# ScalarE's square-root table, the routers' weights on another DMA queue, and products of the identity on TensorE in the first ten microseconds of a transformer block

## The chip, the cores and the metric

The kernel runs on one core of a Trainium2 chip. The metric is the device time of one execution in microseconds. A core has five engines that each work through a queue of instructions in order: TensorE (PE, matmuls and, as PEld, weight loads), VectorE (DVE), ScalarE (ACT), GpSimd (POOL) and SyncE (SP, which here only issues DMAs). ACT and POOL issue DMAs too. In the profile, L110 is line 110 of the kernel.

## What is computed

The reference is one layer in float32 on x of 16 batches, 512 tokens, 256 features. It normalizes each token, and adds to x a linear attention (feature map elu + 1, 16 heads) and a mixture of experts: a shared expert, and 8 routed ones in 2 groups, of which each token takes 2.

```python
xn = _layernorm(x, axis=-1)
x = x + _L0_attn_ref(xn, Wq, bq, Wk, bk, Wv, bv, Wo, bo) \
      + _L0_ffn_ref(xn, w_in, w_out, w1, w2, wg, we, gb, eb)
...
# in _L0_attn_ref
q, k = feature_map(xn @ Wq + bq), feature_map(xn @ Wk + bk)
kv = einsum('bkhd,bkhm->bhdm', k, v)
out = einsum('bqhd,bhdm->bqhm', q, kv) / max(einsum('bqhd,bkhd->bqh', q, k), 1e-6)
...
# in _L0_ffn_ref
g_probs = softmax(flat @ wg.T + gb); e_logits = flat @ we.T + eb
```

`we` (8 columns) and `wg` (2 columns) are the routers' weights.

## The kernel before, in words

A batch of 512 tokens is four tiles of 128 tokens (NT = 4). For every batch the kernel normalizes the tokens (`xn`), brings them into transposed form (`xnT`, the features on the partitions), multiplies by keys and routers in one go (`wkr_sb`: 256 columns of wk, 8 of we, 2 of wg, so 266), then by the queries' weights, and goes on to attention, to the hidden layers of both experts, and to the routing. The main loop (L1034) is staggered: in the turn of batch b the front of batch b + 1 is made (L1038), batch b + 2 is normalized (L1058, `normalize`, statistics at L283), and batch b + 3 is loaded. After all batches, a last stage gathers the tokens of each pair of experts and multiplies them by the second layer (L993).

The change lies in the start:

- L106 `load_x` issues a batch's tokens on SP's queue. L130 loads batch 0 in four pieces, one a tile; L164 loads batch 1 whole, and L1033 batch 2, behind all weights on SP's queue.
- L143 to L145 load we, wg and wk into `wkr_sb`, issued by ACT. L147 takes a square root of a constant, so that the square root's table is loaded early (in the profile a row ACT_TABLE_LOAD of L147).
- L149 loads wq on SP's queue; L151 to L162 load the biases on POOL's; L178 to L193 load the other weights on SP's.
- L300 `first` makes batch 0's and batch 1's start. `measure` (L318) takes mean and variance of a tile on DVE. `scale` takes the root on ACT (L325, `sd`), its inverse and the normalized tile on DVE (L326, L328). `place` (L332) transposes a tile by two products with the identity on PE (L335) and copies it by ACT (L338). `keys` and `queries` are the matmuls through `times` (L342), and `keep` (L355) adds the bias to a result on DVE. L359 to L378 write out their order: tile by tile `measure`, `scale` and the `place` of the tile before, then `keys(0)`, the last tile's `place`, the other keys, the queries, and then the same for batch 1.
- L385 `residual` adds the output bias to the tokens on POOL (L390), and L393 `feature_map` ends in L402.
- The front of batch 1 is `project` (L404): keys at L412, their bias at L416, L417, queries at L423. `summarize` (L684) multiplies the normalized tokens by batch 0's keys (L689); `first_rows` (L636) and `first_hidden` (L655) are the hidden layers of batch 0.

What is passed through `keep_in_program_order` (`pin` in `first`) stays behind what was written before it for its engine. All other instructions are put in order by the compiler's planner, which works with its own estimate of when data come. The semaphores between engines are made by the compiler as well.

Two lines set which instruction of batch 2 stands in DVE's queue early:

```python
with tc.issue_after(last_xn[-1].ins) if last_xn else nullcontext():
    for t in range(g, g + n):
        nc.vector.bn_stats(out=st[:, t, :], in_=xt[:, t, :])
```

So the statistics of batch 2 have to come behind batch 1's last normalized tile, and where behind it is up to the planner.

Of the kernel before, what the change touches and what calls it, by code (L numbers as in the profile page):

```python
# [10 lines left out]
FP = mybir.dt.float32  # L11
# [4 lines left out]
P = 128  # L16
# [5 lines left out]
def block_kernel(  # L22
# [29 lines left out]
    nc = tc.nc  # L52
    B, S, D = x.shape
    G = wg.shape[1]
    E = we.shape[1]
# [5 lines left out]
    NT = S // P  # L61
# [28 lines left out]
    ps_y = ctx.enter_context(tc.tile_pool(name="ps_y", bufs=2, space=bass.MemoryType.PSUM))  # L90
# [12 lines left out]

    hs_all = keep.tile([P, KH, S], FP, name="hs_all")

    def load_x(b, pieces=1):  # L106
        xt = x_all[:, b % 2]
        n = NT // pieces
        for i in range(pieces):
            tc.keep_in_program_order(nc.sync.dma_start(  # L110
                out=xt[:, ts(i, n), :], in_=x[b, ts(i, n * P), :].rearrange("(t p) d -> p t d", p=P)
            ))
        return xt


# [6 lines left out]
    def by_quadrant(a):  # L122
        return a.rearrange("p (q c i) -> p c q i", q=NQ, i=Q)
# [3 lines left out]
    ident = const.tile([P, P], FP)  # L127
    make_identity(nc, ident)

    xs = {0: load_x(0, NT)}  # L130
    KR = D + E + G
    wkr_sb = wp.tile([P, KD, KR], FP)


    w2_sb = wp.tile([P, KH, G * NL * D], FP)
# [3 lines left out]
        first = (LATE + 2 * (i % 2)) * D  # L139
        return w2_sb[:, i // 2, first : first + n * HID]  # L140


    nc.scalar.dma_start(out=wkr_sb[:, :, D : D + E], in_=we.rearrange("(p c) e -> p c e", p=P))  # L143
    nc.scalar.dma_start(out=wkr_sb[:, :, D + E : KR], in_=wg.rearrange("(p c) e -> p c e", p=P))
    nc.scalar.dma_start(out=wkr_sb[:, :, 0:D], in_=wk.rearrange("(p c) f -> p c f", p=P))  # L145
    root = const.tile([P, 1], FP)
    tc.keep_in_program_order(nc.scalar.activation(root, eps_sb, AF.Sqrt))  # L147
# [9 lines left out]
    for q in range(NQ):  # L157
        nc.gpsimd.dma_start(
            out=bv_sb[ts(q, Q)], in_=bv[ts(q, KD * Q)].rearrange("(c i) -> i c", i=Q)
# [3 lines left out]
    if B > 1:  # L163
        xs[1] = load_x(1)  # L164
# [17 lines left out]
    for k in range(KD):  # L182
        for c in range(KD):
            nc.sync.dma_start(
                out=wv_sb[:, k, ts(c, P)].rearrange("p (q i) -> p q i", i=Q), in_=by_quadrant(wv[ts(k, P), :])[:, c]
            )
    wo_sb = wp.tile([P, KD, D], FP)
    for q in range(NQ):
        nc.sync.dma_start(
            out=wo_sb[ts(q, Q)], in_=wo[ts(q, KD * Q), :].rearrange("(c i) d -> i c d", i=Q)  # L190
# [4 lines left out]
    def load_expert(i):  # L195
# [13 lines left out]
        out=headmask, in_=ones, pattern=[[-DH, P // DH], [0, DH]],  # L209
# [3 lines left out]
        out=headmask, in_=headmask, pattern=[[DH, P // DH], [0, DH]],  # L213
# [5 lines left out]
        out=before, in_=ones, pattern=[[1, P]],  # L219
# [80 lines left out]
    def first():  # L300

        pin = tc.keep_in_program_order
        stats = []
        for b in range(2):
            stats.append([
                small.tile([P, NT, n], FP, tag=tag, name=f"{tag}_{b}")  # L310
                for tag, n in (("st", 6), ("mv", 2), ("sd", 1), ("rs", 1))
            ])
        kk, qq = kk_all[:, 0], qq_all[:, 0]
        lg = small.tile([P, NT, E + G], FP, tag="lg", name="lg_0")
        xnT = [work.tile([P, KD, S], FP, tag="xnT", name=f"xnT_{b}") for b in range(2)]
        pks, pqs = [], []

        def measure(b, t):  # L318
            st, mv, _, _ = stats[b]
            pin(nc.vector.bn_stats(out=st[:, t, :], in_=xs[b][:, t, :]))  # L320
            pin(nc.vector.bn_aggr(out=mv[:, t, :], in_=st[:, t, :]))

        def scale(b, t, n):
            _, mv, sd, rs = stats[b]
            pin(nc.scalar.activation(sd[:, t : t + n, 0], mv[:, t : t + n, 1], AF.Sqrt, bias=eps_sb))  # L325
            pin(nc.vector.reciprocal(rs[:, t : t + n], sd[:, t : t + n]))  # L326
            for i in range(t, t + n):
                last_xn[:] = [pin(nc.vector.tensor_scalar(  # L328
                    xn_all[:, b, i, :], xs[b][:, i, :], mv[:, i, 0:1], rs[:, i], ALU.subtract, ALU.mult
                ))]  # L330

        def place(b, t):  # L332
            pt = ps_mm.tile([P, KD, P], FP, tag="mm", name=f"pt_{b}_{t}")
            for c in range(KD):
                pin(nc.tensor.transpose(  # L335
                    pt[:, c, :], xn_all[:, b, t, :].rearrange("p (m c) -> p c m", c=KD)[:, c], ident
                ))
            last_copy[:] = [pin(nc.scalar.copy(xnT[b][:, :, ts(t, P)], pt))]  # L338

        def times(to, t, w):  # L340
            for k in range(KD):
                pin(nc.tensor.matmul(  # L342
                    to, lhsT=xnT[0][:, k, ts(t, P)], rhs=w[:, k, :], start=(k == 0), stop=(k == KD - 1)
                ))

        def keys(t):
            pks.append(ps_mm.tile([P, KR], FP, tag="mm", name=f"pk_0_{t}"))
            times(pks[t], t, wkr_sb)

        def queries(t):  # L350
            if t % 2 == 0:
                pqs.append(ps_y.tile([P, 2, D], FP, tag="py", name=f"pq_0_{t}"))
            times(pqs[-1][:, t % 2, :], t, wq_sb)

        def keep(t):  # L355
            pin(nc.vector.tensor_tensor(kk[:, t, :], pks[t][:, 0:D], bkr_sb[:, 0:D], ALU.add))
            pin(nc.vector.tensor_tensor(lg[:, t, :], pks[t][:, D:KR], bkr_sb[:, D:KR], ALU.add))

        for t in range(NT):  # L359
            measure(0, t)  # L360
            scale(0, t, 1)
            if t:
                place(0, t - 1)
        keys(0)
        place(0, NT - 1)
        for t in range(1, NT):
            keys(t)
        for t in range(NT):
            queries(t)
        for t in range(2):  # L370
            keep(t)
        for t in range(NT):
            measure(1, t)
        for t in range(2, NT):
            keep(t)
        scale(1, 0, NT)
        for t in range(NT):
            place(1, t)  # L378
        for i, pq in enumerate(pqs):
            nc.vector.tensor_tensor(  # L380
                qq[:, 2 * i : 2 * i + 2, :], pq, bq_sb.unsqueeze(1).to_broadcast([P, 2, D]), ALU.add
            )
        return xnT, (qq, kk, lg)
# [638 lines left out]
    waiting = list(range(G * NL))  # L1022

    first_xnT, (qq, kk, lg) = first()
    normed = {b: (xn_all[:, b], first_xnT[b], None) for b in range(2)}
    feature_map(0, kk, "km")
# [4 lines left out]
    fronts = {0: (res, qq, kk)}  # L1031
    queries = {}
    xs[2] = load_x(2)  # L1033
    for b in range(B):  # L1034
        xn, xnT, _ = normed.pop(b)
# [3 lines left out]
        if b + 2 == B:  # L1039

            nc.sync.dma_start(
                out=h_d[ts(b + 1, S), HID:ROW].rearrange("(t p) h -> p t h", p=P), in_=fronts[b + 1][0]
# [59 lines left out]
    n = nc.values_load(  # L1102
        filled, min_val=TT, max_val=TILES,
        skip_runtime_bounds_check_because="whole tiles for all tokens, a part of a tile more for a pair",
    )
# [59 lines left out]
```

## Time and profile before

| | us |
|---|---|
| median of 3 runs | 1040.03 (1039.69 to 1040.49) |
| the profiled execution | 1033.23 |
| its span, first to last instruction | 1031.5 |
| PE busy | 1004.9 |
| DVE busy | 779.4 |
| ACT busy | 488.1 |
| POOL busy | 254.8 |
| tiles of batch 0 issued on SP | 0.82, 1.27, 1.74, 2.24 |
| they landed | 3.00, 4.11, 5.46, 8.17 |
| we, wg, wk issued on ACT | 0.81, 1.49, 2.14 |
| they landed | 3.29, 5.69, 6.50 |

Times in a profile are us from the span's start. A row of the timeline has a start, a duration, the engine, the line, the operation, what it writes and reads, and how many like it follow each other; in brackets is the time for which the engine had been idle, and what ended that. A q behind an engine's name is its sequencer, as for the issue of a DMA. A matmul of float32 operands appears as two instructions, and matmuls overlap, so their spacing tells more than their duration.

### The profile page before, as it was taken

The page shows a single profiled execution, that of the slowest core. Times are in us where ns is not written, and L with a number is a line of the kernel's source. Part 1 is how long each engine was busy: PE and PEld are TensorE (multiplying, and loading weights), DVE is VectorE, ACT ScalarE, POOL GpSimd, SP SyncE. Part 2 cuts the span into 40 slices and gives each one's busy share as a digit, 9 for nine tenths or more (in the row PEclk, how much of TensorE's full clock was granted, in tenths as well). Part 3 has the DMA queues.
Part 4 walks back from the last instruction along what each step waited for, and adds up shares of the span by engine and source line. Part 5 has one row for each costly group of instructions (what it writes and reads, how often), then busy time and mean ns, then how long its engine had stood idle before and what let it go on. Part 6 is the DMA issues. An engine that isn't in the chain of part 4 may idle for free. (4 is left out here: it accounts for less than half of the span.)

```text
span 1031.5 us, 12407 instructions
## 1 busy us (share of the span) xinstructions
PE 1004.9 (97%) x3704; PEld 681.7 (66%) x3704; DVE 779.4 (76%) x1974; ACT 488.1 (47%) x893; POOL 254.8 (25%) x359
## 2 busy tenths in 40 slices
PE   7999999999999999999999999999899999999996
PEld 5466868677786868686777768686667344444442
DVE  5978687878778787878787877868975776666663
ACT  3525353535445253535343534425136576766671
POOL 5302020111202021110202020201012766555652
PEclk9999999999999999999999999999999999999999
DMA  7063534525152522314141313221235755555440
GB/s 220 16 177 107 141 104 101 147 59 154 51 163 54 161 84 81 122 42 143 37 128 56 110 55 123 72 77 61 62 110 146 225 172 153 147 156 157 150 147 30
DMA packets 130339, 116.08 MB, mean 113 GB/s; under 512 B 72637, under 2 KB 114109, under 8 KB 130272
## 3 DMA queue, kind: packets, MB, share of 16 engines
q1 hardware_dynamic: 120064, 77.43, 25.7%
q0 software_dynamic: 9392, 37.58, 12.2%
q8 instruction: 31, 0.51, 0.2%
q10 hardware_dynamic: 816, 0.27, 0.2%
q14 instruction: 36, 0.29, 0.1%
HBM read 65.36 MB, written 50.27 MB: 112 GB/s over the span
## 5 line engine op out<-in xcount | busy, mean ns | idle before, releaser
L993 PE MATMUL py<-w_sb,hT 128*128 x536 | 230.7, 592 | 1.7 <-DVE hT L976 1.6
L993 PEld LDWEIGHTS py<-w_sb,hT 128*128 128x128 f32 x536 | 101.7, 190 | 130.1 <-issue 129.1
L768 PE MATMUL po<-wout_sb,hs_all 128*128 128x256 f32 x480 | 116.6, 380 | 1.4 <-DVE hs_all L580 1.4
L390 POOL TENSOR_TENSOR res<-x_all,bo_sb 128x256 f32<-128x256 f32 x64 | 48.5, 792 | 274.4 <-DMA h_d<-res 203.4
L768 PEld LDWEIGHTS po<-wout_sb,hs_all 128*128 128x128 f32 x480 | 89.2, 190 | 15.1 <-DVE hs_all L580 3.4
L1006 POOL DMA_INDIRECT out<-y,goal x67 | 67.8, 1012 | 76.3 <-DVE y L1003 65.3
L676 POOL TENSOR_TENSOR k<-kk_all 128x512 f32<-128x512 f32 x16 | 20.9, 1307 | 258.3 <-DVE sm L458 247.7
L777 DVE TENSOR_TENSOR res<-po,res 128x256 f32<-128x256 f32 x60 | 25.4, 424 | 76.6 <-PE po L768 76.5
L398 ACT ACTIVATE km<-km 128x1024 f32<-128x1024 f32 x16 | 16.9, 1057 | 138.7 <-DVE km L397 134.4
L595 PE MATMUL phr_w<-w_sb,ss 128*128 128x512 f32 x120 | 61.5, 594 | 2.2 <-DVE ss L538 1.9
L768 PE MATMUL po<-kvo,qT 128*128 128x256 f32 x240 | 61.7, 383 | 0.0
L621 PE MATMUL phs_w<-ss,win_sb 128*128 128x256 f32 x240 | 61.6, 379 | 0.0
L621 PE MATMUL phs_t<-xnT,win_sb 128*128 128x256 f32 x240 | 61.6, 379 | 0.0
L595 PE MATMUL phr_t<-w_sb,xnT 128*128 128x512 f32 x120 | 61.3, 593 | 0.0
L595 PE MATMUL phr_t<-w_sb,ss 128*128 128x512 f32 x120 | 59.4, 597 | 0.0
L621 PE MATMUL phs_t<-ss,win_sb 128*128 128x256 f32 x240 | 59.1, 379 | 0.0
L689 PE MATMUL pxk<-kk_all,xn_all 128*128 128x256 f32 x256 | 58.0, 379 | 0.0
L412 PE MATMUL pk<-wkr_sb,xnT 128*128 128x266 f32 x240 | 57.2, 387 | 0.0
L423 PE MATMUL pq<-w_sb,xnT 128*128 128x256 f32 x240 | 54.2, 379 | 0.0
L689 PEld LDWEIGHTS pxk<-kk_all,xn_all 128*128 128x128 f32 x256 | 48.5, 190 | 6.7 <-issue 0.2
L964 ACT COPY hb<-qq_all 32x256 f32<-32x256 f32 x108 | 43.4, 402 | 17.1 <-DMA qq_all<-h_d,source 9.7
L412 PEld LDWEIGHTS pk<-wkr_sb,xnT 128*128 128x128 f32 x240 | 45.4, 190 | 8.0
(216 smaller groups left out, 1966.0 us busy)
## 6 DMA issues: line engine op xcount, KB each, us to landing
h_d<-hr SPq DMA_DIRECT2D x64, 256.0 KB, 2.5
q_d<-qq_all SPq DMA_DIRECT2D x16, 512.0 KB, 2.8
qb<-q_d SPq DMA_DIRECT2D x64, 128.0 KB, 3.1
w_sb<-in_w SPq DMA_DIRECT2D x64, 128.0 KB, 3.5
h_d<-res SPq DMA_DIRECT2D x60, 129.0 KB, 1.9
x_all<-in_x SPq DMA_DIRECT2D x15, 512.0 KB, 4.8
xn_d<-xn_all SPq DMA_DIRECT2D x14, 512.0 KB, 3.9
xb<-xn_d SPq DMA_DIRECT2D x56, 128.0 KB, 2.8
```

What stands on the lines that cost most here:

```text
L390: nc.gpsimd.tensor_tensor(res[:, t, 0:D], xt[:, t, :], bo_sb, ALU.add)
L412: nc.tensor.matmul(pk, lhsT=xnT[:, k, ts(t, P)], rhs=wkr_sb[:, k, :], start=(k == 0), stop=(k == KD - 1),)
L423: nc.tensor.matmul(pq[:, t, :], lhsT=xnT[:, k, ts(t2 + t, P)], rhs=wq_sb[:, k, :], start=(k == 0), stop=(k == KD - 1),)
L595: tc.keep_in_program_order(nc.tensor.matmul(to, lhsT=xs7[i][:, ts(u, P)], rhs=w1_in[W7[i]], start=start, stop=stop, skip_group_check=True,))
L621: tc.keep_in_program_order(nc.tensor.matmul(split(to)[:, f, :], lhsT=win_in[W7[i]][:, ts(2 * u + f, P)], rhs=xs7[i], start=start and f == ...
L676: nc.gpsimd.tensor_tensor(k2, kk[:, 0:2, :], kk[:, 2:4, :], ALU.add)
L689: nc.tensor.matmul(pxk[:, c, :], lhsT=xn[:, t, ts(c, P)], rhs=kk[:, t, :], start=(t == 0), stop=(t == NT - 1),)
L768: nc.tensor.matmul(po, lhsT=a, rhs=w, start=(i == 0), stop=(i == len(parts) - 1))
L777: nc.vector.tensor_tensor(res[:, t, 0:D], po, res[:, t, 0:D], ALU.add)
L964: nc.scalar.copy(there[ts(q, Q), a - near, 0:n, :], self.hg[ts(a, Q), 0:n, ts(q, W)])
L993: nc.tensor.matmul(py.rearrange("p j d -> p (j d)"), lhsT=self.hT[:, f, ts(j, P)], rhs=w2_sb[:, f, bass.ds(regs[i % TR], 2 * D)], start=(f ...
L1006: stored = nc.gpsimd.indirect_dma_start(out=out_rows, out_offset=bass.IndirectOffsetOnAxis(ap=self.goal[:, i : i + 1], axis=0), in_=y, in_ ...
```

## The change

The routers' weights are no longer issued by ACT. SP issues them, between the second and the third tile of batch 0's tokens, pinned to that place. ACT keeps wk's load and then the root of the constant. TensorE gets products of the identity by itself, into a PSUM tile that nobody reads: seven ahead of the first transposes, and two behind each of the first three tiles' transposes. They are pinned too. The PSUM tile takes one of the two buffers with the tag py, which the queries' results of this stage use next.

```diff
-    def load_x(b, pieces=1):
+    def load_x(b, pieces=1, then={}):
         xt = x_all[:, b % 2]
         n = NT // pieces
         for i in range(pieces):
             tc.keep_in_program_order(nc.sync.dma_start(
                 out=xt[:, ts(i, n), :], in_=x[b, ts(i, n * P), :].rearrange("(t p) d -> p t d", p=P)
             ))
+            if i in then:
+                then[i]()
         return xt
...
-    xs = {0: load_x(0, NT)}
     KR = D + E + G
     wkr_sb = wp.tile([P, KD, KR], FP)
+
+    def load_routers():
+        for w, at, n in ((we, D, E), (wg, D + E, G)):
+            tc.keep_in_program_order(nc.sync.dma_start(
+                out=wkr_sb[:, :, at : at + n], in_=w.rearrange("(p c) e -> p c e", p=P)
+            ))
+
+    xs = {0: load_x(0, NT, {1: load_routers})}
...
-    nc.scalar.dma_start(out=wkr_sb[:, :, D : D + E], in_=we.rearrange("(p c) e -> p c e", p=P))
-    nc.scalar.dma_start(out=wkr_sb[:, :, D + E : KR], in_=wg.rearrange("(p c) e -> p c e", p=P))
     nc.scalar.dma_start(out=wkr_sb[:, :, 0:D], in_=wk.rearrange("(p c) f -> p c f", p=P))
...
+        def warm(n):
+
+            for _ in range(n):
+                pin(nc.tensor.matmul(idle, lhsT=ident, rhs=ident, start=True, stop=True))
+
+        idle = ps_y.tile([P, P], FP, tag="py", name="idle")
+        warm(7)
         for t in range(NT):
             measure(0, t)
             scale(0, t, 1)
             if t:
                 place(0, t - 1)
+                warm(2)
         keys(0)
         place(0, NT - 1)
```

## The prediction

> **What bounds the kernel now.** I read the page first, for the engine that is full:
>
> ```profile
> span 1031.5 us, 12407 instructions
> PE 1004.9 (97%) x3704; PEld 681.7 (66%) x3704; DVE 779.4 (76%) x1974; ACT 488.1 (47%) x893; POOL 254.8 (25%) x359
> ```
>
> PE is idle for 26.6 us of the span, and the change touches only the start. A gain in the start is worth something only if nothing behind it ends a wait at a time of its own. So the second view is the timeline of the first 60 us (start, duration, engine and line; in brackets idle time and what ended it):
>
> ```profile
> 2.81 1.28 ACT L147 ACT_TABLE_LOAD   x1 [2.81 <-issue]
> ...
> 3.03 0.43 DVE L320 BATCH_NORM_STATS2 st<-x_all 128x6 f32<-128x256 f32 x1 [3.03 <-DMA x_all<-in_x]
> ...
> 4.21 0.28 ACT L325 ACTIVATE sd<-mv,eps_sb 128x1 f32<-128x1 f32 x1
> ...
> 8.97 1.98 PE L342 MATMUL pk<-wkr_sb,xnT 128*128 128x266 f32 x4
> ...
> 14.69 3.62 PE L342 MATMUL pq<-w_sb,xnT 128*128 128x256 f32 x16
> ...
> 20.03 0.42 SPq L110 DMA_DIRECT2D x_all<-in_x  x1
> ...
> 24.78 0.43 DVE L283 BATCH_NORM_STATS2 st<-x_all 128x6 f32<-128x256 f32 x1 [2.48 <-DMA x_all<-in_x]
> ...
> 26.18 1.22 DVE L402 SCALAR_TENSOR_TENSOR kk_all<-kk_all,km 128x1024 f32<-128x1024 f32 x1
> ...
> 27.54 3.69 PE L689 MATMUL pxk<-kk_all,xn_all 128*128 128x256 f32 x16
> ...
> 51.22 1.98 PE L663 MATMUL phs<-xnT,win_sb 128*128 128x512 f32 x4 [1.54 <-DVE hr L651]
> ```
>
> The row at 24.78 decides the case. DVE, which takes its instructions in order, stands for 2.48 us until batch 2's tokens land (issued at 20.03). Behind that wait stand three of the four `keep` steps of batch 1 and L402, and PE's `pxk` waits for L402's keys (27.40). Does DVE have air after that? The view by windows (PE, PEld, DVE busy first) and the list of waits say no:
>
> ```profile
> 24.78:51.20 26.42, 24.75 (x74) 13.46 (x72) 26.31 (x99) 13.00 (x15) 9.31 (x14) 1.00 0.03 11
> ```
>
> ```profile
> DVE st L283 <- DMA x_all<-in_x: 2.5, 1, 2.5
> ```
>
> DVE is busy 26.31 of 26.42 us from that landing to 51.20, and there PE waits 1.54 us for DVE's `hr`. Later PE runs almost without a gap. So the chain that sets the end starts with the landing of x(2), goes through DVE to 51.22, and then through PE. What is won before 24.78 only lengthens the wait there.
>
> **The change part by part.**
>
> *Two DMA issues off ACT's queue.* They took 0.64 and 0.63 us there (at 0.81 and 1.49); wk's issue moves from 2.14 to 0.81, and the table load from 2.81 to about 1.48, ending at 2.76, root at 2.97. The first variance is ready at 3.49 + 0.18 = 3.67, so sd would start at 3.71 instead of 4.21: 0.50 us won, if tile 0 still lands at 3.00.
>
> *wk's transfer 1.33 us earlier.* It now shares the DMA engines with tiles 0 and 1. Their packets (1 KB) took 46 ns each, 8 per engine and tile. The Trainium skill (DMA: Bandwidth & Descriptors, Queues, rings and completion order) says each DMA engine takes turns between the queues that have work, packet by packet. By the row alone (tile 0 beside the tiny routers' packets) nothing is lost; by the rule tile 0 waits for as many of wk's packets: 8 x 46 ns = 0.37 us. Below: -0.1, since the routers' 256 packets of 9 ns no longer run beside it (0.14 us over 16 engines). Above: wk's first 30 packets took 280 to 415 ns, two per engine, so 0.37 + 0.8 = 1.2. I take 0.37, the ordinary packet. Of 0.50 remain 0.13 us for the whole loop over four tiles, which runs at 1.53 us a tile through DVE and ACT.
>
> *Two issues onto SP's queue, past tiles 2 and 3, wq, batch 1 and all weights.* An issue of a tile took 0.40 to 0.61 us there; with gaps the two cost about 1.2 us. Tile 2 was issued at 1.74, landed at 5.46 and was wanted at 6.58: at +1.2 it is just in time. Tile 3 was issued at 2.24, landed at 8.17 and was wanted at 8.34, now 8.2. By its row it lands with the crowd on the engines, not a fixed time after its issue (5.9 us against 2.2 for tile 0): between no delay and 1.2 us. I take none, since wk is out of the way by then; at worst DVE stands 1.15 us. For the loads behind, SP's own waits matter (in the trace an issue waits for the landing of a DMA some eight before it):
>
> ```profile
> SPq L184 <- DMA w_sb<-in_w: 2.0, 1, 2.0
> SPq L179 <- DMA wkr_sb<-in_wg: 1.0, 1, 1.0
> ...
> SPq L184 <- DMA x_all<-in_x: 0.8, 1, 0.8
> ```
>
> L179's issue at 5.70 had waited 1.0 us for wg's landing. With everything 1.2 us later it comes at 5.25 + 0.7 = 5.95 with nothing to wait for: 0.25 us late, not 1.2. The two waits of L184 are for landings of batch 1 (11.72) and of w1 (14.24), on DMA engines whose busy share was about 1.0 from 10 to 17 us; the same bytes go through them in nearly the same order. So x(2) is issued 0 to 0.25 us later and lands at about 24.96: **+0.2 us**, from -0.3 to +1.2 (the whole delay kept).
>
> *Thirteen products of the identity.* ident is ready at 2.57 (POOL). PE's spacing in the trace is 0.444 us for a 266-column matmul up to 12.5 us and 0.2235 us from 12.9 on, although the column of the granted clock shows 1.00 in both; so a 128-column half costs 0.214 or 0.108 us, and a product is two of them. Seven cost 14 x 0.214 = 3.0 us, until 5.6; the first transposes were due at 5.1 and slip 0.5 us, which only ACT's copy of tile 0 feels (due 5.99, the next sd behind it at 7.1). Two before the keys cost 0.43 us fast or 0.85 slow, on PE's path. Does the rate double before the keys? By the row it came 4.4 us after unbroken work began at 8.48. The Trainium skill (TensorE: Matmul & The Clock Gate, Part 1) tells of a gate that opens after a busy window of some 3.4 us and whose windows run free: from 2.6 us on that gives 6.0 to 9.4. Its Part 4 speaks against the change: transposes don't count as busy, so the stretches between the products could be too thin. No row here separates these. Open: keys(0) at 8.84 + 0.43 = 9.27, its four halves 0.89, two transposes about 0.4, twelve halves of keys(1..3) 2.68: the queries start at 13.25, not 14.69, 1.4 us won. Shut: 0.85 - 0.13 = 0.7 lost. I take open, nearer to both row and rule.
>
> *Up to 24.78.* Of 1.4 us, 0.4 goes at L328: three of its four rows ran at 0.81 to 1.0 us beside POOL's residual (13.90 to 19.55, held by bo's landing, which the change leaves), against 0.40 alone; now all four do. So batch 1's keys start about 1.0 us earlier, at 19.5. DVE reaches L283 at 21.3, not 22.3, and waits 3.7 us instead of 2.48. PE ends its queries at about 26.7 and waits some 0.9 us for L402: a new wait takes the place of the old ones. Cover: the start may even be 2.4 us later than now before the end moves. Without this cover, the win would reach the end up to 1.0 us.
>
> *Sum.* 1031.5 + 0.2 = 1031.7 us of span, 1033.4 with the 1.7 us around it (1033.23 before). The median of the runs shown is 1040.03, 6.8 us above the profiled execution; I carry the difference over: 1040.2 us. Under 0.2%, 2.1 us, a measurement of this kernel can't tell a change from none.
>
> **The rivals.**
>
> *The wait for x(2) leaves DVE's path: faster.* L283 isn't pinned; the planner put it there. Two loads more on SP can make it think that x(2) comes later and set L283 behind some `keep` steps (0.55 us won for each) or behind L402. Then DVE is up to 2.48 + 1.0 us earlier, PE by its own 1.0 plus the 1.69 us that it idled between 45.8 and 51.2: the smaller, 2.7 us, gives 1037.3. For it: an addition for a later batch, L538, stands ahead of L283, so the planner thought x(2) not landed a few steps earlier; the decision is near. Against: the same near decision can move it by just one step. Chance 0.3: 0.2 for over 2.1 us, 0.1 for a part.
>
> *SP's delay reaches x(2): slower.* The place is the row at 20.03. If the 1.0 us wait of L179 doesn't absorb the two issues, because in the new order another late landing stands eight DMAs ahead of it, x(2) comes 1.2 us later; if batch 1's load (landed 11.72) and with it the two waits of L184 lose a second such step, 2.4 us. Every ns of it goes through DVE to 51.22: 1041.2 to 1042.4. It decides beyond 0.2% when x(2) lands after 26.9. For it: x(2) stands last behind 17 other issues of that queue. Against: engines full from 10 to 17 us. Chance 0.25, of it 0.15 beyond 0.2%.
>
> *The products do not open the gate.* 0.7 us late in the start, hidden at 24.78: 1040.2 too. It is inside the first case.
>
> **How the numbers follow.** Order and landing kept, within 0.2%: 0.45, 1040.2 (1039.7 to 1040.9). With the parts of the rivals under the bound (0.1 each) same is 0.65; faster 0.2; slower 0.15. The range reaches into both rivals, from 1037.5 to 1042.0, and leaves out about 0.1 on each side.
>
> **What would show it.** Right: the table load at 1.5; 266-column matmuls 0.22 us apart from keys(0) on; queries from 13.3; L283's wait grown to about 3.7 us with x(2) landing near 25.0; PE's `pxk` waiting for L402; the rows from 27.5 to 51.2 at their old times. Wrong: L283 behind L402, x(2) landing beyond 26, or an order on DVE or PE after 28 us that differs from before.

## The result and the profile after

The changed kernel takes 1042.2 us (median, 1041.17 to 1044.08), the kernel before 1040.03 (1039.59 to 1041.16), 19 runs of each: the ratio is 1.0019, with an interval of 1.0013 to 1.0026. That is 2.2 us slower, where 1040.2 had been forecast, and 0.2 us above the upper end of the forecast range (1042.0). The profiled execution of the changed kernel took 1042.67 us, and its span is 1041.0.

That span is not to be compared with the 1031.5 us shown for before. The kernel before was profiled a second time (e0 below), and there the span is 1038.6. The first profile lacks a wait of some 4.9 us on PE near 825 us that all other profiles of this case have. So the late stages are compared with e0, and the first 75 us with both.

The page of the changed kernel has the same full engine. PE has 26 instructions more, two for each of the thirteen products:

```profile
span 1041.0 us, 12457 instructions
PE 1012.0 (97%) x3730; PEld 688.4 (66%) x3730; DVE 777.4 (75%) x1974; ACT 488.0 (47%) x893; POOL 255.1 (25%) x359
```

The timeline of its first 80 us, with the rows that answer to those of the prediction:

```profile
1.48 1.28 ACT L153 ACT_TABLE_LOAD   x1 [1.48 <-PEq L1166]
...
2.62 3.36 PE L368 MATMUL idle<-ident 128*128 128x128 f32 x14 [2.62 <-POOL ident masks.py:199]
3.01 0.43 DVE L326 BATCH_NORM_STATS2 st<-x_all 128x6 f32<-128x256 f32 x1 [3.01 <-DMA x_all<-in_x]
3.69 0.29 ACT L331 ACTIVATE sd<-mv,eps_sb 128x1 f32<-128x1 f32 x1 [0.71 <-DVE mv L327]
...
9.12 0.43 DVE L326 BATCH_NORM_STATS2 st<-x_all 128x6 f32<-128x256 f32 x1 [2.96 <-DMA x_all<-in_x]
...
10.79 0.51 PE L341 MATMUL pt<-ident,xn_all 128*128 128x128 f32 x2 [2.50 <-DVE xn_all L334]
...
11.82 1.98 PE L348 MATMUL pk<-wkr_sb,xnT 128*128 128x266 f32 x4
...
20.98 0.42 SPq L110 DMA_DIRECT2D x_all<-in_x  x1
...
26.51 0.43 DVE L289 BATCH_NORM_STATS2 st<-x_all 128x6 f32<-128x256 f32 x1 [4.17 <-DMA x_all<-in_x]
...
30.18 2.18 PE L703 MATMUL pxk<-kk_all,xn_all 128*128 128x256 f32 x9 [1.50 <-DVE sm L472]
...
66.69 0.42 DVE L736 TENSOR_TENSOR vk<-vk,headmask 128x256 f32<-128x256 f32 x1
...
67.17 1.13 PE L745 MATMUL pm<-wo_sb,vk 128*128 128x256 f32 x4 [0.87 <-DVE vk L736]
...
76.77 3.53 PE L426 MATMUL pk<-wkr_sb,xnT 128*128 128x266 f32 x15
```

Three things are to be seen. The head start works: the table is loaded at 1.48, tile 0's root starts at 3.69 (4.21 before). Then tile 2, wanted at 6.16, lands at 9.12, so that the first keys start at 11.82, 2.85 us later than before (8.97). And this delay, too, ends in the wait for batch 2's tokens, which grew from 2.48 to 4.17 us. What is behind it is late by the landing (26.51 for 24.78 and, in e0, 25.29) and by something more, since `pxk` starts 2.1 to 2.6 us later, not 1.2 to 1.7.

The "something more" is in DVE's order. These are rows of DVE around its wait, first of e0 (before), then of after:

```profile
21.21 0.41 DVE L538 TENSOR_TENSOR ss<-xnT 128x256 f32<-128x256 f32 x1
21.54 0.18 DVE L449 TENSOR_TENSOR ex<-lg,mx 128x32 f32<-128x32 f32 x1
21.64 0.15 DVE L452 TENSOR_TENSOR ex<-lg,mx 128x8 f32<-128x8 f32 x1
21.72 0.41 DVE L416 TENSOR_TENSOR kk_all<-pk,bkr_sb 128x256 f32<-128x256 f32 x1
22.05 0.15 DVE L417 TENSOR_TENSOR lg<-pk,bkr_sb 128x10 f32<-128x10 f32 x1
25.29 0.43 DVE L283 BATCH_NORM_STATS2 st<-x_all 128x6 f32<-128x256 f32 x1 [3.09 <-DMA x_all<-in_x]
```

```profile
26.51 0.43 DVE L289 BATCH_NORM_STATS2 st<-x_all 128x6 f32<-128x256 f32 x1 [4.17 <-DMA x_all<-in_x]
26.85 0.18 DVE L463 TENSOR_TENSOR ex<-lg,mx 128x32 f32<-128x32 f32 x1
26.95 0.16 DVE L466 TENSOR_TENSOR ex<-lg,mx 128x8 f32<-128x8 f32 x1
27.02 0.42 DVE L430 TENSOR_TENSOR kk_all<-pk,bkr_sb 128x256 f32<-128x256 f32 x1
27.36 0.16 DVE L431 TENSOR_TENSOR lg<-pk,bkr_sb 128x10 f32<-128x10 f32 x1
...
42.14 0.41 DVE L552 TENSOR_TENSOR ss<-xnT 128x256 f32<-128x256 f32 x1
```

Before, five instructions (L538, L449, L452 and batch 1's first `keep`, L416 and L417) were done ahead of the wait, in time that DVE had to spare. In the changed kernel the planner set batch 2's first statistic ahead of the same five (L552, L463, L466, L430, L431), and they are done behind the landing. DVE has no gap from the landing to the last product for `vk` (L722 before, L736 after): 39.10 us in before, 39.08 in e0, 40.18 after. The five take 1.30 us by their durations in e0 and about 0.9 by the spacing of their rows there; the measured difference is 1.09. These are the rows of before that the comparison rests on:

```profile
6.58 0.42 DVE L320 BATCH_NORM_STATS2 st<-x_all 128x6 f32<-128x256 f32 x1
...
63.88 0.43 DVE L722 TENSOR_TENSOR vk<-vk,headmask 128x256 f32<-128x256 f32 x1
...
73.96 3.76 PE L412 MATMUL pk<-wkr_sb,xnT 128*128 128x266 f32 x16
```

From there on no difference follows the kernel. In every profile of this case, before's two, after's two and the ten of edited kernels, the keys of batch 2 (L412, in after L426) start 10.07 to 10.09 us after that instruction for `vk`, and except in before's first profile the span ends 963.8 to 965.5 us after those keys. They start at 73.96 in before, at 74.45 in e0 and at 76.77 in after. So a profile of this case can be judged by one row, the start of batch 2's keys, to within the 1.7 us by which the rest varies.

### The profile page after: what moved, and what is told of

It reads as the page before. It is cut to its first block, busy times and chain, and to the rows that moved or that the text cites. A ratio compares the mean times of both kernels' runs of the same rounds, so it can differ in the third digit from the quotient of the medians.

```text
span 1041.0 us, 12457 instructions
## 1 busy us (share of the span) xinstructions
PE 1012.0 (97%) x3730; PEld 688.4 (66%) x3730; DVE 777.4 (75%) x1974; ACT 488.0 (47%) x893; POOL 255.1 (25%) x359
## 5 line engine op out<-in xcount | busy, mean ns | idle before, releaser
L782 PE MATMUL po<-wout_sb,hs_all 128*128 128x256 f32 x480 | 118.9, 385 | 2.1 <-DVE hs_all L594 1.4
L412 ACT ACTIVATE km<-km 128x1024 f32<-128x1024 f32 x16 | 16.9, 1057 | 138.3 <-DVE km L411 134.0
L426 PE MATMUL pk<-wkr_sb,xnT 128*128 128x266 f32 x240 | 57.2, 387 | 0.0
L426 PEld LDWEIGHTS pk<-wkr_sb,xnT 128*128 128x128 f32 x240 | 45.4, 190 | 8.0
```

The costliest lines, as they stand in the source:

```text
L426: nc.tensor.matmul(pk, lhsT=xnT[:, k, ts(t, P)], rhs=wkr_sb[:, k, :], start=(k == 0), stop=(k == KD - 1),)
L782: nc.tensor.matmul(po, lhsT=a, rhs=w, start=(i == 0), stop=(i == len(parts) - 1))
```

## The experiments

Of all twelve runs this table gives the median with its ratio to the kernel before, run beside it (interval in brackets; e9 and e10 were run once, and have none), and from the profile the time at which tile 2's statistic started, at which batch 2's first statistic started (which is x(2)'s landing where DVE waited for it), and at which batch 2's keys started. None of the kernels leaves out or changes a part of what is computed. Kernels are best compared by the ratio, for the kernel before took 1040.03 us beside after, 1040.71 beside e0 to e3, 1040.13 beside e4 to e7 and 1040.32 beside e8 and e11.

| | us | ratio | tile 2 | statistic of batch 2 | batch 2's keys |
|---|---|---|---|---|---|
| before | 1040.03 | | 6.58 | 24.78, waited 2.48 | 73.96 |
| e0 before again | 1040.82 | 1.0002 [0.9995, 1.0008] | no wait | 25.29, waited 3.09 | 74.45 |
| after | 1042.2 | 1.0019 [1.0013, 1.0026] | 9.12 | 26.51, waited 4.17 | 76.77 |
| e9 after again | 1041.74 | | 9.06 | 25.87, waited 3.65 | 76.12 |
| e1 no products | 1038.07 | 0.9976 [0.9968, 0.9985] | 9.01 | 32.63, no wait | 72.37 |
| e2 products only | 1042.17 | 1.0016 [1.0009, 1.0022] | no wait | 27.09, waited 7.35 | 77.76 |
| e10 products only again | 1042.85 | | no wait | 25.67, waited 6.06 | 75.90 |
| e3 routers after tile 3 | 1042.35 | 1.0016 [1.001, 1.0023] | no wait | 26.12, waited 5.67 | 76.37 |
| e8 few packets | 1042.08 | 1.0016 [1.0009, 1.0022] | 6.58 | 25.65, waited 5.72 | 76.36 |
| e4 after, pinned | 1039.73 | 0.9989 [0.998, 0.9997] | 9.23 | 34.04, no wait | 73.78 |
| e5 before, pinned | 1037.5 | 0.9973 [0.9962, 0.9984] | no wait | 30.83, no wait | 70.58 |
| e6 products, pinned | 1036.29 | 0.9965 [0.9951, 0.9978] | no wait | 30.42, no wait | 70.07 |
| e7 tile 3, pinned | 1037.03 | 0.9967 [0.9955, 0.9979] | no wait | 30.36, no wait | 70.10 |
| e11 tokens ahead of wo | 1037.39 | 0.9973 [0.9964, 0.9983] | no wait | 20.83, no wait | 71.17 |

Two theories stood at first: that the place of the wait in DVE's queue and the landing of x(2) set the end (the queue), or that the late tile 2 and what it delays do (the front).

### e0: the kernel before once more

No edit.

> The kernel before, unchanged, for a second profile of it and for the spread between two copies. By every theory 1040.0 us (1039.6 to 1040.6). Theory QUEUE (the change loses its time by a late landing of batch 2's tokens, which goes through DVE) and theory FRONT (it loses it because PE stands 2.5 us for tile 2 and all that follows shifts) expect the same rows as in the first profile up to 700 us. Theory END (part of the loss comes behind 700 us from the change) expects PE without the two waits of 4.9 and 1.3 us around 815 to 827 us that the changed kernel shows; if the copy shows them too, they are no effect of the change.

The time agrees with before's, run beside it (1040.71, ratio 1.0002); both lie a little above the range that was expected. Its profile shows how far two profiles of one kernel lie apart: x(2) landed at 25.29 instead of 24.78, and batch 2's keys came 0.49 us later. From the landing to `vk` they agree within 0.02 us.

### e1: the change without the products

```diff
-        idle = ps_y.tile([P, P], FP, tag="py", name="idle")
-        warm(7)
...
-                warm(2)
```

> The change without its thirteen products: the routers are on SP's queue, ACT's table load is early. The planner now puts batch 2's statistics behind the step that ends batch 0's keys. QUEUE: tile 2 still lands late (DVE waits about 3 us near 9 us) and the first keys run at half rate, batch 2's tokens still land near 26.5, but DVE no longer waits for them; the products of batch 0's keys start near 29 us, PE-bound, and part of this is made good at 51 us: 1040.5 to 1041.5 us. FRONT: as slow as the change plus the slow keys, 1042.7 us or more.

A miss, and on the good side: 1038.07, faster than both. Tile 2 was as late as in after (9.01), but the planner set batch 2's statistics behind L402 (here L413) and even behind the start of `pxk` (28.40):

```profile
24.59 1.22 DVE L413 SCALAR_TENSOR_TENSOR kk_all<-kk_all,km 128x1024 f32<-128x1024 f32 x1
...
32.63 0.42 DVE L289 BATCH_NORM_STATS2 st<-x_all 128x6 f32<-128x256 f32 x1
```

No wait for x(2) is left. PE runs from `pxk` to batch 2's keys in 43.97 us without waiting, against 46.42 in before. This is the prediction's faster rival, which the products had undone in the whole change.

### e2 and e10: the products alone

The kernel before with `warm`, the tile `idle` and the calls of the change; the DMAs and the table's load stay as they were. e10 is the same kernel again.

> The kernel before with the thirteen products alone: the routers stay on ACT's queue. The planner puts three of batch 2's statistics, and two subtractions behind the first, ahead of the step that ends batch 0's keys, as in the changed kernel. QUEUE: tile 2 lands as before (near 5.5), the first keys run at full rate and start about 1 us earlier, batch 2's tokens land at 24.8 as before, and what the planner put behind that wait costs 0.9 to 1.3 us: 1041.0 us (1040.6 to 1041.4). FRONT: the start is 1 us shorter and nothing is late, 1039.0 to 1040.0 us.

> The products alone again, for a second profile. SP's queue is that of the kernel before, yet batch 2's tokens came at 27.1 instead of 24.8 to 25.3. If they come at 27 again, the products delay the landing by some path not seen yet; if they come near 25, the landing spreads by 2 us between executions, and the products' cost is the planner's order alone.

1042.17: within the intervals of the two ratios (1.0016 and 1.0019) the products alone cost what the whole change costs. This is over the range of the queue theory, too, since x(2) landed late. The front was early (first keys at 9.26, queries at 13.09) and tile 2 on time, so the theory of the front falls. DVE's order is after's, with the statistic ahead of the five instructions, although no DVE instruction was edited. From the landing to `vk` DVE took 40.59 us in e2 and 40.15 in e10, after's 40.18 again. x(2) landed late here too, at 27.09 and 25.67, with SP's queue as in before; 1.4 us lie between two profiles of one kernel.

### e3: the routers' weights behind tile 3

```diff
-    xs = {0: load_x(0, NT, {1: load_routers})}
+    xs = {0: load_x(0, NT, {3: load_routers})}
```

> The change with the routers' weights behind all four tiles of batch 0 on SP's queue instead of behind the second. QUEUE: tiles 2 and 3 land in time (no wait of DVE near 9 us), the first keys come about 1 us earlier than before unless they wait for the routers' weights, but batch 1's and batch 2's tokens are still late (batch 2 near 26), so the time stays near the change: 1041.3 to 1042.2 us. FRONT: the loss is gone, 1039.0 to 1040.0 us.

Tiles 2 and 3 were on time, PE's first keys came at 9.97, 1.85 us earlier than in after, and the time is the same, 1042.35 (0.15 above the range of the queue theory). The front's gain went into the wait for x(2), which grew to 5.67 us.

### e4 to e7: the statistics held behind batch 0's keys

One line sets where the planner may put batch 2's statistics (the list is what the `issue_after` of the statistics looks at):

```diff
-    feature_map(0, kk, "km")
+    last_xn[:] = [feature_map(0, kk, "km")]
```

e4 is after with it, e5 before, e6 the products alone, e7 e3 with it.

> The changed kernel with batch 2's statistics pinned behind the step that ends batch 0's keys, so that DVE's order no longer depends on the planner's guess. ORDER (the kernel pays for what stands behind DVE's wait for batch 2's tokens; the place of that wait was moved by the products in the planner's order): DVE doesn't wait for batch 2 any more, PE runs without a gap from batch 1's keys (21.5 us) to 440 us, about as without products: 1038.2 us (1037.4 to 1039.0), 2 us or more faster than before and 4 faster than the change. LANDING (the time goes where a late landing goes, wherever the wait stands): at most the two subtractions and one statistic are won, 1041.0 to 1042.0 us.

> The kernel before with that one pin. ORDER: DVE's wait of 2.5 to 3 us is gone, PE goes on at 20.4 us without a gap: 1037.4 us (1036.7 to 1038.2), 0.9 us better than the changed kernel with the pin, since its tile 2 isn't late. LANDING: 1039.5 to 1040.7 us.

> The products alone (routers on ACT's queue) with the pin. ORDER: now the earlier start reaches the end, because nothing waits in between: batch 1's keys at 18.8 us against 20.4, so 1035.8 us (1035.0 to 1036.8), the fastest of these. LANDING: 1039.5 to 1041 us.

> The change with the routers behind tile 3 and with the pin. ORDER: batch 1's keys at 19.5 us as in the same kernel without the pin, so between the two others: 1036.5 us (1035.7 to 1037.4). LANDING: 1039.5 to 1041.5 us.

e5 shows the price of the wait in the kernel before: 2.6 us (1037.5 beside 1040.13). With the wait gone, PE goes from `pxk` to batch 2's keys in 43.97 to 44.18 us in all four, so what is won in the front now reaches the end. e6 is the fastest of all kernels, 3.8 us under before, 1.2 under e5 (their intervals overlap); e7 is equal to it, so the table's earlier load, with the routers behind tile 3, brought nothing that can be measured. e4, the whole change, keeps only 0.4 us, where 1.9 had been expected: 3.4 us more than e6. The view by windows of e4 (PE, PEld, DVE, ACT, POOL busy, granted clock, DMA share, GB/s) shows half of the clock in two windows, the first of which begins while PE waits for tile 2 (3.20 us, until 10.90):

```profile
10.10:13.50 3.40, 2.60 (x9) 2.37 (x10) 1.67 (x6) 0.94 (x4) 0.39 (x1) 0.50 0.97 288
13.50:16.90 3.40, 3.40 (x10) 2.57 (x9) 0.93 (x5) 0.37 (x1) 3.40 (x6) 0.50 1.07 376
```

Batch 1's keys started at 22.75 in e4, at 18.84 in e6. In e1, which lacks the products and has tile 2 as late and the statistics behind `pxk` too, they started at 21.34, and it took 1038.07 us. So beside a late tile 2 the products showed no gain, and more likely a loss (the intervals of e1 and e4 overlap).

### e8: few packets in the routers' place

Are the two issues on SP what makes tile 2 late, or the routers' small packets? Here we and wg are issued by ACT again, and SP gets two loads of 16 rows of 512 bytes into a tile that nobody reads, in the same place.

```diff
-        for w, at, n in ((we, D, E), (wg, D + E, G)):
-            tc.keep_in_program_order(nc.sync.dma_start(
-                out=wkr_sb[:, :, at : at + n], in_=w.rearrange("(p c) e -> p c e", p=P)
-            ))
+        for i in range(2):
+            tc.keep_in_program_order(nc.sync.dma_start(out=stand_in[:, i, :], in_=wo[ts(i, 16), 0:128]))
```

> The change, but in the routers' place on SP's queue stand two loads of 16 rows of 512 bytes into a tile that nobody reads (the same two issues, 32 packets instead of 512); the routers are back on ACT's queue ahead of wk, so ACT's table load is late again. DVE's order is the planner's, with three statistics ahead, as in the change. PACKETS (the routers' small packets hold SP's queue for about 2 us): tile 2 lands about 1.2 us later than before the change, near 6.7, DVE's wait near 9 us is gone or under 0.7 us, and the products keep TensorE's rate up from the first keys on. ISSUES (the two issues are enough): tile 2 lands near 9 as in the change. The total stays at 1041 to 1042.3 us by both, since DVE still waits for batch 2's tokens.

Tile 2's statistic started at 6.58 without a wait, as in before. The row of the window 3.5 to 6.5 us, first after, then e8:

```profile
3.50:6.50 3.00, 3.00 (x16) 3.00 (x16) 1.82 (x7) 0.65 (x3) 3.00 (x7) 1.00 0.64 70
```

```profile
3.50:6.50 3.00, 3.00 (x16) 3.00 (x16) 1.65 (x7) 1.34 (x5) 3.00 (x7) 1.00 0.99 166
```

With the routers' 512 packets (256 of 32 and 256 of 8 bytes) in front of tile 2, the DMA engines moved 70 GB/s at a busy share of 0.64; with 32 packets of 512 bytes in their place 166 GB/s (before: 180 at 0.95). So it is the packets and not the issues; whether their number or their size counts, e8 doesn't separate. Nor is it the time of their transfers: by the trace's records of packets each took 9 ns, 0.28 us in all over 16 engines, and the last ended at 5.37. The first packet of tile 2, by the order of the queue, started at 5.65 in after, at 4.83 in e8 and at 3.46 in before, and from 5.30 on 4 KB packets of POOL's bias loads ran beside tile 2, which in before started at 7.13, behind it. What the queue spends between the small packets no run shows. The total didn't move (1.0016), since the wait for x(2) took this gain as well.

### e9: the changed kernel once more

> The changed kernel again, for a second profile: how much of the late tile 2 (9.1 us) and of batch 2's late landing (26.5 us) comes again. PACKETS: tile 2 lands at 8.9 to 9.3 again. If batch 2's landing comes within 0.6 us of 26.5 it belongs to the kernel; if it moves by 1 us or more it is mostly a spread between executions.

x(2) landed at 25.87 (26.51 in the first profile) after 5.26 us of flight (5.53). That is 0.64 us of difference, between the two bounds that had been set, and decides nothing. Tile 2 came late again (9.06), as expected. From the landing to `vk` DVE took 40.16 us.

### e11: tokens of batch 2 ahead of wo and w_out

The kernel before, with SP's loads of wo and w_out moved behind batch 2's tokens:

```diff
     xs[2] = load_x(2)
+    for q in range(NQ):
+        tc.keep_in_program_order(nc.sync.dma_start(
+            out=wo_sb[ts(q, Q)], in_=wo[ts(q, KD * Q), :].rearrange("(c i) d -> i c d", i=Q)
+        ))
+    tc.keep_in_program_order(nc.sync.dma_start(out=wout_sb, in_=w_out.rearrange("(c p) d -> p c d", p=P)))
```

> The kernel before with batch 2's tokens issued on SP's queue ahead of wo's and w_out's loads instead of behind them; everything else as before, no products, no pin. The planner again sets three statistics ahead of the step that ends batch 0's keys. WAIT (only the wait at the landing costs, the order by itself does not): batch 2 is issued near 16.7 and lands near 21 us, DVE doesn't stand at L278 or for under 0.5 us, and the time falls as with the pin: 1037.6 us (1036.8 to 1038.5). STATISTICS (what costs is three statistics ahead of the keys): 1040.5 to 1041.3 us.

Is it the wait that costs, or the statistics that stand early on DVE?

```profile
20.83 0.41 DVE L278 BATCH_NORM_STATS2 st<-x_all 128x6 f32<-128x256 f32 x1
...
23.24 1.22 DVE L397 SCALAR_TENSOR_TENSOR kk_all<-kk_all,km 128x1024 f32<-128x1024 f32 x1
...
27.05 3.62 PE L684 MATMUL pxk<-kk_all,xn_all 128*128 128x256 f32 x16
```

Three statistics stand in after's place in DVE's queue, ahead of L397, and the row at 20.83 has no bracket: the tokens, issued at 16.25 and not at 20.03, are there. The kernel is 2.9 us faster (1037.39 beside 1040.32). So by standing early the statistics cost nothing that can be measured; the wait does.

## Why the prediction was off by two microseconds

**Right: what sets the end.** The prediction put everything on the row at 24.78: what is won before it only lengthens the wait, and the landing of x(2) goes on to the end. e2, e3 and e8 won up to 4 us in the front against after (queries at 13.09, 13.88 and 13.42 for 17.07) and ended within 0.2 us of it (ratios of 1.0016 beside 1.0019).

**Right in kind, cut short: the chain behind the landing.** It said "through DVE to 51.22, and then through PE". In after PE doesn't wait for `hr` near 51 us at all; it waits between 64 and 67.2, for `hs_all` and `vk`. DVE had no gap up to `vk` at 63.88 in before either, and PE's weight load waited 0.35 us for it there. The error cost no time in the sum, but hid that work moved behind the wait counts as far as 64 us.

**Wrong: "Order and landing kept".** This step failed twice.

- *The order.* The prediction knew that L283 isn't pinned and that the decision was near, but weighed only that the planner would set it later. It set it earlier, ahead of five instructions: +1.08 us between the means of the two pairs of profiles (before and e0, after and e9), a term that the sum doesn't have. Which edit did it is settled: with products the statistic comes ahead of the five (after, e2, e3, e8), without them but with the DMAs moved it comes behind L402 (e1), with neither in the place of before. Moved DMAs alone can also bring it forward (e11), so the direction is the planner's and not to be read off the edit.
- *The landing of x(2).* I took +0.2 us, with bounds from -0.3 to +1.2. Measured were 26.51 and 25.87 beside 24.78 and 25.29: +1.16 between the means, of which 0.47 is the later issue and 0.69 a longer flight. That L179's wait of 1.0 us absorbs the two issues was right: the loads of wv were issued at 10.42 in after, at 10.17 in before and 10.68 in e0. But batch 1's tokens, issued 1.1 us later, then landed late for them (0.8 us before):

```profile
SPq L190 <- DMA x_all<-in_x: 3.0, 1, 3.0
```

  This is the slower rival's second step ("if batch 1's load ... loses"). But x(2) was late in e2 and e10 too (27.09, 25.67), where SP's queue is as in before. How much of the 1.16 belongs to the queue, to the products or to the scatter of x(2)'s flight (4.5 to 6.9 us where DVE waited) stays open.

Together 1.08 + 1.16 = 2.24 us; batch 2's keys start 2.24 us later between the same means, and the medians differ by 2.2. So the two terms account for the loss, but why x(2) came late is not shown. The prediction also held that under 0.2% this kernel's time can't be told from no change; with 19 runs of each, 0.19% could (1.0013 to 1.0026).

**Wrong, and hidden: tile 2 "just in time".** The two issues on SP were costed as 1.2 us of issuing. What counts is what stands in them, 512 small packets, behind which tile 2 landed at 9.12: DVE stood 2.96 us, where the sum had at worst 1.15 (for tile 3). In after the wait for x(2) covers it. Between e4 and e6, where that cover is gone, the whole change costs 3.4 us more than the products alone, and e7, with the routers behind tile 3, only 0.7.

**Right: tile 0 and the table.** Table at 1.48 and sd at 3.69 (1.48 and 3.71 forecast with an unhindered tile). Tile 0 was there at 3.01: wk's transfer didn't delay it, so the 0.37 us taken from the Trainium skill's rule of turns between queues (DMA: Bandwidth & Descriptors) were too much here. The two transfers hardly met: of wk's 256 packets 34 started before the last of tile 0's, at 2.60. So the rule itself was not put to the test. (The 280 to 415 ns behind the forecast's upper bound are means: of wk's first 30 packets in before 16 took 46 ns and the others 138 to 1133.)

**Half right: the gate.** The clock rose at 7.9 us in after, within the 6.0 to 9.4 that were worked out, and at 5.8 to 8.1 in the kernels with the products; in those without them at 11.3 to 15.1. So they suffice. Whether transposes count (the Trainium skill, TensorE: Matmul & The Clock Gate, Part 4) stays open: the first seven products alone fill PE from 2.62 to 5.98, and in e7 the rate rose at 5.76, when the first transpose had only just begun (5.77). Where tile 2 is on time the forecast of the front holds: in e2 the first keys start at 9.26 and the queries at 13.09 (9.27 and 13.25 forecast). But in the whole change "open for the keys" didn't hold, because PE stood 2.50 us for tile 2 and the clock went back to half from 11.3 to 14.7. The queries start at 17.07 with the products and at 16.94 without them (e1). This view of after by windows has the granted clock as the third value from the end:

```profile
7.90:11.30 3.40, 0.91 (x7) 0.72 (x7) 1.70 (x6) 0.56 (x2) 1.55 (x22) 1.00 1.07 371
11.30:14.70 3.40, 3.40 (x12) 2.76 (x12) 1.07 (x4) 0.93 (x3) 0.87 (x2) 0.50 1.02 349
```

**Near by luck: the price of the faster rival.** 1037.3 was worked out for the wait's leaving DVE's path; e5 measured 1037.5, e11 1037.39, e1 1038.07. But of the 2.7 us in that sum 1.0 was the front's gain by the change, and none of these three kernels has that gain by its edit: without the wait alone 2.6 to 2.9 us are won, not 1.7. With the products' front on top it is 3.8 (e6), and with the whole change, whose tile 2 is late, 0.4 (e4).

## What to carry to other kernels

When one engine waits for a transfer and what stands behind it goes to the end without a gap, look at which instructions stand ahead of the waiting one: if a planner orders them, any edit, even on another engine, can move the wait by a few places in either direction, so both directions belong in the forecast, and the place is best pinned. A gain ahead of such a wait is worth nothing until the wait is gone; remove that first, then measure the others (e5 before e6). Cost a DMA that is moved in front of others by its packets, not only by its issue: many small ones held up what stood behind them for far longer than their own transfers took (0.28 us here).

## What the runs showed of the hardware

- Small packets hold up what is queued behind them: behind 512 packets, 10 KB in all, DVE waited 2.96 us for tile 2; behind two issues of 32 packets and 16 KB in the same place it didn't wait (e8).
- With the clock at full, a wait of 2.5 us and more on PE brought half of it for one or two windows of 3.4 us: 2.50 us in after (11.3 to 14.7), and 4.71 us in e2, where an earlier front makes PE wait longer at `pxk`. A wait of 1.50 us, at `pxk` in after, left it at 1.00. The rows of e2:

```profile
29.90:33.30 3.40, 2.54 (x6) 2.12 (x7) 3.39 (x11) 2.11 (x2) 2.03 (x2) 0.50 0.00 0
33.30:36.70 3.40, 3.40 (x9) 2.69 (x9) 3.38 (x12) 0.00 (x0) 0.00 (x0) 0.50 0.00 0
```

  In e2 and e8, with two such windows, it took DVE 0.45 us more from the landing to `vk` than in e3 and e10, with one.
- The granted clock reads 1.00 until the first change that the trace records, although matmuls of 266 columns stand 0.444 us apart there and 0.2235 later. In the first microseconds the spacing tells the rate, not that column.
